# A four-layer conditioned sequence kernel: start of the scans, order of the attention's products, place of the last SiLU

## The chip, the core and the metric

The kernel runs on one core of a Trainium2 chip, in one launch. The metric is the time on the device in microseconds (us), the median of several runs. Engine names are those of the profile: PE multiplies matrices (PEld are its weight loads), DVE, ACT and POOL work on elements, SP issues the DMAs. All data is float32.

## What is computed

Two sequences of 1024 positions with 256 features go through four layers, each with a residual and each shifted and scaled by a condition vector:

```python
x = L0(x, c)     # layer norm, in-projection, conv of 4 taps, SiLU, selective scan, SiLU gate, out-projection
x = L1(x, c)     # two layer norms, two selective scans (one over the reversed sequence), SiLU gates
x = L2(x, e)     # attention with softmaxes over features of q and over positions of k: k^T v first
x = L3(x, e)     # full softmax attention: 16 heads of 16 features over 1024 positions
# a selective scan, for 512 channels x 16 states:
h = h * exp(dt * A) + (dt * u) * B ;  y = sum_n(h * C)
# the end of L2 and L3:
h = layer_norm(y) * (1 + scale) + shift ;  x = x + silu(h) @ W + b
```

## The kernel before

**Order of the work.** The body is written under a manual schedule, which starts at line 1515: each engine runs its instructions in the order in which Python traces them. The constants above it (lines 144 to 203: columns, masks, `negA`, the SiLU of the condition) are placed by the scheduler. Three stages follow each other.

**Prologue.** `layer0(0)` is traced until the first block of dt is saved: layer norm of two tiles of 512 positions (`normed`, with `root` for 1/sqrt by Ln and Exp on ACT, `refine` on DVE, `scaled` on ACT), flips to channels and their eviction with the condition's scale and shift (`channels`), the in-projection and a conv of four taps (three `scalar_tensor_tensor` on DVE for each of four blocks of channels, line 674), SiLU (`smooth`), the projection to dt, B and C (`ssm_inputs`) and softplus. Between the layer norm and the flips stand the condition's matmuls (`cond_first`, `cond_cols`) and their columns (`affine`). ACT needs different tables of functions for SiLU and for Ln and Exp; `preload_act_table_set` (line 203 and line 684) loads one that has both Ln and Exp.

**Scans.** `chain` goes through six scans of 32 pairs of tiles. A tile holds 32 channels x 4 states by 1024 positions. For each: `load_spread` brings dt and dt*u from DRAM (`sp`), `load_bc` B and C (`bc`), ACT makes exp(dt*A) (`decay`, line 931), POOL dt*u*B (`inputs`, line 936), DVE scans (lines 943 and 947) and multiplies with C (line 950) or leaves that to POOL (line 949), and PE sums over states into `ys_t` (`fold`, line 974). Before the first pair, lines 1019 to 1032 load the first tiles in the order spread 0, bc 0, spread 1, bc 1 to 3, and make the first decay and three inputs. The other layers' work is cut into generators that `Behind` runs between the tiles within a budget of matmul columns, ACT and POOL time. `later` and `save` delay a DMA by a number of these slots; in the prologue, `until` issues all that is delayed at its next turn.

**Tail.** `attention` computes L3's softmax attention and runs the last generators behind it. A step handles, for a group of four heads, one tile of 128 keys against 512 queries. It is cut into two parts. In each part PE makes four scores (line 1418): two whose exponentials ACT takes out of PSUM (line 1497) into `hb_t`, and two of a group 12 steps ahead (`LAG`), whose maxima DVE takes (line 1427). Scores go into a pool of seven banks (`sc`); the eighth bank, `av`, collects the products of exponentials with v, 32 rows for each of the four heads. After its scores, each part issues the products of the step before for half of the columns:

```python
for j in range(4):
    at = (j % 2) * 512 + part * 256
    nc.tensor.matmul(
        sums.av[32 * j : 32 * j + 32, ts(part, 256)],
        sts[b]["v"][t // 2][:, t % 2, 4 * g + j, :], es[j // 2][:, at : at + 256],
        start=(t == 0 and part == 0), stop=(t == NT - 1 and part == 1),
    )
```

Then one step of a background generator follows (`behind.slot(1)`), so such work can stand between the halves of a step. When a half of a sequence is done, `last` flips it back, divides by the sums, and `stylize` ends the layer: layer norm, flips, eviction with scale and shift as Identity, SiLU in place over each of two tiles (`channels`, `silu`, which loads the table of Ln and Exp again), the out-projection and the residual (line 791).

The profile gives one line for helpers: L133 is `act_f`, L95 is `mm`, L99 is `flip`, L120 is `save`.

Of the kernel before, what the change touches and what calls it, by code (L numbers as in the profile page):

```python
# [12 lines left out]
AF = mybir.ActivationFunctionType  # L13
# [5 lines left out]
P = 128  # L19
# [35 lines left out]
def kernel(ctx: ExitStack, tc: tile.TileContext, a: dict, out: bass.AP):  # L55
# [146 lines left out]
    act_f(sc, cT, AF.Silu)  # L202
    nc.scalar.preload_act_table_set("natural_log_exp_and_others")

# [48 lines left out]
    def affine(mod, scale_at, shift_at, g, bias, name):  # L253

        s = const.tile([P, 2, B], F32, tag=f"{name}s", name=f"{name}s")
        o = const.tile([P, 2, B], F32, tag=f"{name}o", name=f"{name}o")
        for c in range(2):
            g_c, b_c = col(g, c), col(bias, c)
            at = mod[:, scale_at + c, :]
            act_f(s[:, c, :], at, AF.Identity, bias=g_c, scale=g_c)  # L260
            t = small_t((P, B), "aff")
            act_f(t, mod[:, shift_at + c, :], AF.Identity, bias=b_c)
            for b in range(B):
                act_f(
                    o[:, c, b : b + 1], at[:, b : b + 1], AF.Identity,
                    bias=t[:, b : b + 1], scale=b_c,
                )
        return s, o
# [155 lines left out]

    def scaled(src, r, q):
        o = abuf((P, 4, D))
        for j in range(4 if mode["tail"] else 0):
            nc.vector.tensor_scalar(
                o[:, j, :], src[:, j, :], r[:, j : j + 1], q[:, j : j + 1], ALU.mult, ALU.add
            )  # L430
        for j in range(0 if mode["tail"] else 4):
            act_f(
# [5 lines left out]
    def normed(src, res):  # L438
# [9 lines left out]
        for i, t in enumerate(src):  # L448
            res.append(scaled(t, r[:, ts(i, 4)], q[:, ts(i, 4)]))
            yield  # L450
# [6 lines left out]

    def channels(src, dst, func, scale, bias, halves=(0, 1)):

# [6 lines left out]

        def take(i, c, ps):
            act_f(
                dst[c][:, ts(i, 512)], ps, AF.Identity, bias=bias(c), scale=scale(c)
            )  # L470
# [4 lines left out]
        ))  # L475
        if func is AF.Silu:
            done = slice(512 * halves[0], 512 * halves[-1] + 512)
# [78 lines left out]
    def ssm_inputs(key, u, w_xp, w_dt, dt_b, st):  # L556
# [15 lines left out]
        if key == "00":  # L572
            pss = [bank() for _ in range(2)]
            for k in range(4):
                for ch in range(2):
# [3 lines left out]
                    )  # L579
            take(0, pss[0])  # L580
            nc.vector.tensor_copy(dbl[:, 512:], pss[1][: R + 2 * N, :])
        else:
# [3 lines left out]
        st["bc"] = dbuf((2 * N, T), f"bc_{key}")  # L586
        save(2, st["bc"], dbl[R : R + 2 * N, :])


# [286 lines left out]
    class Scan:  # L876
# [56 lines left out]

        def inputs(self, c, k):
            e = hb()
            nc.gpsimd.tensor_tensor(e, self.sp[c, 1], self.bc[0][k], ALU.mult)  # L936
            return e
# [53 lines left out]
    def chain(scans, rates, early, mid, after):  # L991
# [29 lines left out]
        for w in range(2):  # L1021
            s.load_spread(0, w)
        s.load_bc(0)
        for w in range(2):
# [4 lines left out]
        ahead(0, "decay")  # L1029
        ahead(0, "inputs")  # L1030
        ahead(1, "inputs")
# [62 lines left out]

    def stylize(b, y, aff, w_o, bias, src, dst, halves=(0, 1), to=None):

# [3 lines left out]
        yield from normed(y, yn)  # L1100
        y.clear()
        hT = [abuf() for _ in range(2)]
        yield from channels(
            yn, hT, AF.Silu, lambda c: s[:, c, b : b + 1], lambda c: o[:, c, b : b + 1], halves
        )
# [266 lines left out]
    def last(b, st, src, i):  # L1372
# [22 lines left out]
        ))  # L1395
        yield from stylize(b, y, "aff3", w_o, row("bo3"), src, out[b], (i,))

    def attention(sts, done):
# [50 lines left out]

        def sums(part, n, step, es):  # L1450

            b, g = groups[n]
            ch, t = divmod(step, NT)
            if t == 0 and part == 0:
                sums.av = bank("av")
            for j in range(4):
                at = (j % 2) * 512 + part * 256
                nc.tensor.matmul(  # L1458
                    sums.av[32 * j : 32 * j + 32, ts(part, 256)],
                    sts[b]["v"][t // 2][:, t % 2, 4 * g + j, :], es[j // 2][:, at : at + 256],  # L1460
                    start=(t == 0 and part == 0), stop=(t == NT - 1 and part == 1),
                )
            if t == NT - 1 and part == 1:
                if ch == 0:
# [6 lines left out]
        for at in range(steps + LAG):  # L1471
# [8 lines left out]
            for part in range(2):  # L1480
# [12 lines left out]
                for kind, j, ps in made:  # L1493
                    if kind:
                        top(n1, step1, j, ps)
                    else:
                        act_f(es[j // 2][:, ts(j % 2, 512)], ps, AF.Exp)
                if late is not None:
                    sums(part, *late)
                    if part == 1 and late[0] % 4 == 3 and late[1] % NT == NT - 1:  # L1500
                        done(late[0] // 4, late[1] // NT)
                    if part == 1:
                        late = None
                behind.slot(1)
            if has_e:
                late = (n, step, es)
        for part in range(2):
            sums(part, *late)
        done(B - 1, 1)
# [4 lines left out]
    x3 = [dbuf((T, D), f"x3{b}") for b in range(B)]  # L1514
    ctx.enter_context(tc.manual_schedule())
    sts = [{"v": [], "qk": [], "y": []} for _ in range(B)]
    with ExitStack() as s:
# [4 lines left out]
        psum.append(s.enter_context(tc.tile_pool(name="psS", bufs=1, space=bass.MemoryType.PSUM)))  # L1522
        s00 = Scan("00", negA[0], "D0", False, True)
        s01 = Scan("01", negA[0], "D0", False, True)
        s10 = Scan("10", negA[1], "D1", False, False)
# [194 lines left out]
```

## Time and profile before

| | |
|---|---|
| median of 3 runs | 2122.8 us (2117.06 to 2125.97) |
| profiled execution | 2117.43 us |
| its span, first to last instruction | 2115.4 us |
| busy in the span | PE 1626.8, DVE 1745.5, POOL 1356.9, ACT 1140.4 us |
| granted TensorE clock, mean | 0.833 |
| first scan starts | 69.5 us |
| first and last score | 1479.0 and 2088.6 us |

A row of the profile's timeline is: start in us, duration in us, engine, line, operation, output<-inputs by the program's names, shapes, and how many instructions are merged in it; in brackets how long the engine was idle before it and what ended that. One matmul in float32 stands as two instructions in PE's rows. Ends of PE's rows are modelled, so the distance from the start of one row to the start of the next says more than a row's duration. Parts of the span are named by its time in us.

### The profile page before, as it was taken

The page shows a single profiled execution, that of the slowest core. Times are in us where ns is not written, and L with a number is a line of the kernel's source. Part 1 is how long each engine was busy: PE and PEld are TensorE (multiplying, and loading weights), DVE is VectorE, ACT ScalarE, POOL GpSimd, SP SyncE. Part 2 cuts the span into 40 slices and gives each one's busy share as a digit, 9 for nine tenths or more (in the row PEclk, how much of TensorE's full clock was granted, in tenths as well). Part 3 has the DMA queues.
Part 4 walks back from the last instruction along what each step waited for, and adds up shares of the span by engine and source line. Part 5 has one row for each costly group of instructions (what it writes and reads, how often), then busy time and mean ns, then how long its engine had stood idle before and what let it go on. Part 6 is the DMA issues. An engine that isn't in the chain of part 4 may idle for free.

```text
span 2115.4 us, 22775 instructions
## 1 busy us (share of the span) xinstructions
PE 1626.8 (77%) x8112; PEld 617.7 (29%) x8112; DVE 1745.5 (83%) x1728; ACT 1140.4 (54%) x1583; POOL 1356.9 (64%) x667
## 2 busy tenths in 40 slices
PE   6576867288697547886945658944999899999997
PEld 3132313033141202222312323300545333333333
DVE  4688898898999999998999987998767757777763
ACT  5565666375546345764555453542044555656665
POOL 0789898898999999999998977998101211000000
PEclk9688968599796558988977865965899999999999
DMA  3663458245653555555653344332300111020001
GB/s 111 239 222 114 157 184 292 83 157 185 254 196 141 179 172 187 189 179 188 250 206 110 117 159 144 123 132 73 116 1 1 39 21 18 23 56 1 2 1 38
DMA packets 106870, 267.53 MB, mean 126 GB/s; under 512 B 14618, under 2 KB 39067, under 8 KB 106756
## 3 DMA queue, kind: packets, MB, share of 16 engines
q1 hardware_dynamic: 106756, 266.07, 37.1%
q8 instruction: 64, 1.05, 0.2%
q14 instruction: 50, 0.41, 0.1%
HBM read 195.90 MB, written 67.90 MB: 125 GB/s over the span
## 4 chain that ended last, share of the span: by engine, by line
PE 30%; DVE 10%; POOL 5%; issue 4%; ACT 2%; DMA 0%; DVEq 0%; ACTq 0%; POOLq 0%
PE sc_t L1418 13%; PE av_t L1458 6%; PE sc_t L95 4%; POOL hb_t L936 3%; PE bank_t L95 3%; DVE dA_t L943 2%; DVE mh L1427 2%; PE sc_t L99 2%; DVE dA_t L947 2%; POOL hb_t L949 1%; PE ys_t L974 1%; DVE hb_t L943 1%; ACT act_t L133 1%; POOL act_t L141 1%; DVE hb_t L947 1%
## 5 line engine op out<-in xcount | busy, mean ns | idle before, releaser
L936 POOL TENSOR_TENSOR hb_t<-sp,bc 128x1024 f32<-128x1024 f32 x384 | 908.8, 2399 | 88.5 <-PE ys_t L974 52.0
L133 ACT ACTIVATE dA_t<-sp,negA 128x1024 f32<-128x1024 f32 x384 | 428.5, 1117 | 548.3 <-DVE hb_t L950 432.8
L947 DVE TENSOR_TENSOR_SCAN dA_t<-dA_t,hb_t 128x1024 f32<-128x1024 f32 x195 | 445.9, 2287 | 62.3 <-ACT dA_t L133 35.1
L1427 DVE TENSOR_REDUCE mh<-sc_t 128x1 f32<-128x512 f32 x512 | 327.5, 686 | 110.2 <-PE sc_t L1418 109.8
L974 PE MATMUL ys_t<-hb_t,fold 128*32 128x512 f32 x1536 | 294.2, 781 | 153.5 <-POOL hb_t L949 101.1
L133 ACT ACTIVATE hb_t<-sc_t 128x512 f32<-128x512 f32 x512 | 276.9, 595 | 188.7 <-PE sc_t L1418 188.5
L950 DVE TENSOR_TENSOR hb_t<-dA_t,bc 128x1024 f32<-128x1024 f32 x285 | 349.1, 1225 | 21.4 <-DVE dA_t L947 0.5
L1418 PE MATMUL sc_t<-act_t 32*128 32x512 f32 x2048 | 336.6, 650 | 11.0 <-DVE mh L1427 7.3
L949 POOL TENSOR_TENSOR hb_t<-hb_t,bc 128x1024 f32<-128x1024 f32 x99 | 235.7, 2381 | 19.6 <-DVE hb_t L947 17.8
L784 POOL TENSOR_TENSOR act_t<-act_t,row 128x1024 f32<-128x1024 f32 x8 | 18.7, 2347 | 339.9 <-PE sc_t L99 193.3
L943 DVE TENSOR_TENSOR_SCAN dA_t<-dA_t,hb_t 128x1024 f32<-128x1024 f32 x90 | 205.7, 2285 | 9.2 <-POOL hb_t L936 6.0
L1458 PE MATMUL av_t<-hb_t,act_t 128*32 128x256 f32 x2048 | 164.3, 393 | 1.1 <-DVE act_t L1466 1.1
L95 PE MATMUL bank_t<-act_t,w_c_w 128*128 128x512 f32 x256 | 129.6, 657 | 41.2 <-ACT act_t L133 41.2
L133 ACT ACTIVATE act_t<-bank_t,cols 128x512 f32<-128x512 f32 (+1 forms) x206 | 129.9, 677 | 44.5 <-PE bank_t L95 38.7
L1418 PEld LDWEIGHTS sc_t<-act_t 32*128 32x128 f32 x2048 | 111.1, 185 | 120.9 <-issue 79.9
L974 PEld LDWEIGHTS ys_t<-hb_t,fold 128*32 128x32 f32 x1536 | 40.5, 123 | 358.9 <-POOL hb_t L949 139.5
L947 DVE TENSOR_TENSOR_SCAN hb_t<-dA_t,hb_t 128x1024 f32<-128x1024 f32 x61 | 139.0, 2279 | 3.9 <-ACT dA_t L133 3.6
L141 POOL TENSOR_TENSOR act_t<-act_t 128x1024 f32<-128x1024 f32 x50 | 118.4, 2367 | 0.2
L99 PE MATMUL bank_t<-ident,act_t 128*128 128x128 f32 x128 | 34.6, 426 | 92.5 <-ACT act_t L133 92.3
L95 PE MATMUL bank_t<-act_t,w_dt_w 64*128 64x512 f32 x96 | 74.6, 912 | 40.4 <-ACT act_t L133 34.4
L1458 PEld LDWEIGHTS av_t<-hb_t,act_t 128*32 128x32 f32 x2048 | 42.1, 108 | 190.5 <-issue 177.8
L1363 POOL MEMSET act_t<- 128x1024 f32 x8 | 7.6, 952 | 128.0 <-PE sc_t L1418 128.0
(176 smaller groups left out, 1833.9 us busy)
## 6 DMA issues: line engine op xcount, KB each, us to landing
sp<-dt SPq DMA_DIRECT2D x192, 512.0 KB, 5.3
dt<-act_t SPq DMA_DIRECT2D x48, 512.0 KB, 5.2
bc<-bc SPq DMA_DIRECT2D x48, 512.0 KB, 7.7
u<-act_t SPq DMA_DIRECT2D x24, 512.0 KB, 5.0
fu<-u SPq DMA_DIRECT2D x24, 512.0 KB, 4.5
y<-y SPq DMA_DIRECT2D x96, 128.0 KB, 5.8
g<-act_t SPq DMA_DIRECT2D x16, 512.0 KB, 5.3
fg<-g SPq DMA_DIRECT2D x64, 128.0 KB, 4.7
```

What stands on the lines that cost most here:

```text
L95: nc.tensor.matmul(o, w, x, **kw)
L133: nc.scalar.activation(o, x, func, **kw)
L141: nc.gpsimd.tensor_tensor(o, x, y, op)
L936: nc.gpsimd.tensor_tensor(e, self.sp[c, 1], self.bc[0][k], ALU.mult)
L943: nc.vector.tensor_tensor_scan(h[:, ::-1], dA[:, ::-1], e[:, ::-1], 0.0, ALU.mult, ALU.add)
L947: nc.vector.tensor_tensor_scan(h, dA, e, 0.0, ALU.mult, ALU.add)
L949: return lambda: nc.gpsimd.tensor_tensor(e, h, self.bc[1][k], ALU.mult)
L950: nc.vector.tensor_tensor(e, h, self.bc[1][k], ALU.mult)
L974: nc.tensor.matmul(self.ys[d, cp][at : at + DS, :], fold, e[:, ts(ch, 512)], start=False, stop=(k == NK - 1),)
L1418: nc.tensor.matmul(ps, w[r, ts(at, P)], x[r, ts(wide_at, 512)], start=True, stop=True)
L1427: nc.vector.tensor_reduce(mh[n][:, t, ch, j : j + 1], ps, AX.X, ALU.max)
L1458: nc.tensor.matmul(sums.av[32 * j : 32 * j + 32, ts(part, 256)], sts[b]["v"][t // 2][:, t % 2, 4 * g + j, :], es[j // 2][:, at : at + 256] ...
```

## The change

It has three parts. In the prologue, the preload of the table moves from behind the condition's SiLU to the first place under the manual schedule; while no scans run yet, the columns of `affine`, the scaling of the second tile, the eviction of the second block of channels and both copies of the projection are done by DVE instead of ACT; the load of the first B and C is issued behind their save, before dt is saved; the first product dt*u*B is made by DVE. In the attention, the products of the step before are issued once a step, behind the second part's scores, over 512 columns. In the very last `stylize`, a SiLU of one column is issued after the layer norm, the eviction applies SiLU itself, and the separate SiLUs and the reload of the table are left out.

```diff
--- before.py
+++ after.py
@@ -200,7 +200,6 @@
 
     sc = const.tile([P, 4, B], F32, tag="sc", name="sc")
     act_f(sc, cT, AF.Silu)
-    nc.scalar.preload_act_table_set("natural_log_exp_and_others")
 
     def small_t(shape, tag, bufs=2):
         return small.tile(list(shape), F32, tag=tag, name=tag, bufs=bufs)
@@ -257,6 +256,14 @@
         for c in range(2):
             g_c, b_c = col(g, c), col(bias, c)
             at = mod[:, scale_at + c, :]
+            if not mode["scans"]:
+                t = small_t((P, B), "aff")
+                nc.vector.tensor_scalar(t, at, 1.0, None, ALU.add)
+                nc.vector.tensor_scalar(s[:, c, :], t, g_c, None, ALU.mult)
+                nc.vector.scalar_tensor_tensor(
+                    o[:, c, :], t, b_c, mod[:, shift_at + c, :], ALU.mult, ALU.add
+                )
+                continue
             act_f(s[:, c, :], at, AF.Identity, bias=g_c, scale=g_c)
             t = small_t((P, B), "aff")
             act_f(t, mod[:, shift_at + c, :], AF.Identity, bias=b_c)
@@ -422,13 +429,14 @@
         e.scalar_tensor_tensor(q, mv[:, :, 0], -1.0, r, ALU.mult, ALU.mult)
         return q
 
-    def scaled(src, r, q):
+    def scaled(src, r, q, i):
         o = abuf((P, 4, D))
-        for j in range(4 if mode["tail"] else 0):
+        far = mode["tail"] or i and not mode["scans"]
+        for j in range(4 if far else 0):
             nc.vector.tensor_scalar(
                 o[:, j, :], src[:, j, :], r[:, j : j + 1], q[:, j : j + 1], ALU.mult, ALU.add
             )
-        for j in range(0 if mode["tail"] else 4):
+        for j in range(0 if far else 4):
             act_f(
                 o[:, j, :], src[:, j, :], AF.Identity,
                 bias=q[:, j : j + 1], scale=r[:, j : j + 1],
@@ -446,7 +454,7 @@
         q = refine(mv, r)
         yield
         for i, t in enumerate(src):
-            res.append(scaled(t, r[:, ts(i, 4)], q[:, ts(i, 4)]))
+            res.append(scaled(t, r[:, ts(i, 4)], q[:, ts(i, 4)], i))
             yield
 
     def silu(t):
@@ -455,7 +463,7 @@
         nc.scalar.preload_act_table_set("natural_log_exp_and_others")
         spent["ACT"] += 2400
 
-    def channels(src, dst, func, scale, bias, halves=(0, 1)):
+    def channels(src, dst, func, scale, bias, halves=(0, 1), ready=False):
 
 
         def turn(i, c):
@@ -465,15 +473,21 @@
             return ps
 
         def take(i, c, ps):
+            if c and not (mode["scans"] or mode["tail"]):
+                nc.vector.tensor_scalar(
+                    dst[c][:, ts(i, 512)], ps, scale(c), bias(c), ALU.mult, ALU.add
+                )
+                return
             act_f(
-                dst[c][:, ts(i, 512)], ps, AF.Identity, bias=bias(c), scale=scale(c)
+                dst[c][:, ts(i, 512)], ps, func if ready else AF.Identity,
+                bias=bias(c), scale=scale(c),
             )
 
         yield from pipe(*(
             (lambda i=i, c=c: turn(i, c), lambda ps, i=i, c=c: take(i, c, ps))
             for i in halves for c in range(2)
         ))
-        if func is AF.Silu:
+        if func is AF.Silu and not ready:
             done = slice(512 * halves[0], 512 * halves[-1] + 512)
             act_f(dst[0][:, done], dst[0][:, done], func)
             silu(dst[1][:, done])
@@ -577,14 +591,16 @@
                         pss[ch][: R + 2 * N, :], w_xp[:, k, :], u[k][:, ts(ch, 512)],
                         start=(k == 0), stop=(k == 3),
                     )
-            take(0, pss[0])
-            nc.vector.tensor_copy(dbl[:, 512:], pss[1][: R + 2 * N, :])
+            for ch in range(2):
+                nc.vector.tensor_copy(dbl[:, ts(ch, 512)], pss[ch][: R + 2 * N, :])
         else:
             yield from pipe(*(
                 (lambda ch=ch: low(ch), lambda ps, ch=ch: take(ch, ps)) for ch in range(2)
             ))
         st["bc"] = dbuf((2 * N, T), f"bc_{key}")
         save(2, st["bc"], dbl[R : R + 2 * N, :])
+        if "first" in st:
+            later(2, st["first"])
 
 
         st["dt"] = dbuf((2, DI, T), f"dt_{key}")
@@ -931,9 +947,9 @@
             act_f(dA, self.sp[c, 0], AF.Exp, scale=self.nA[:, at : at + 1])
             return dA
 
-        def inputs(self, c, k):
+        def inputs(self, c, k, engine=nc.gpsimd):
             e = hb()
-            nc.gpsimd.tensor_tensor(e, self.sp[c, 1], self.bc[0][k], ALU.mult)
+            engine.tensor_tensor(e, self.sp[c, 1], self.bc[0][k], ALU.mult)
             return e
 
         def tile(self, c, k, dA, e, far=False):
@@ -1020,14 +1036,13 @@
         behind.until(lambda: s.st["have"])
         for w in range(2):
             s.load_spread(0, w)
-        s.load_bc(0)
         for w in range(2):
             s.load_spread(1, w)
         for k in range(1, NK):
             s.load_bc(k)
         s.load_rest(0)
         ahead(0, "decay")
-        ahead(0, "inputs")
+        made["inputs"][0] = s.inputs(0, 0, nc.vector)
         ahead(1, "inputs")
         ahead(2, "inputs")
         mode["scans"] = True
@@ -1092,16 +1107,20 @@
         scans[-1].finish(3, 1)
         flush()
 
-    def stylize(b, y, aff, w_o, bias, src, dst, halves=(0, 1), to=None):
+    def stylize(b, y, aff, w_o, bias, src, dst, halves=(0, 1), to=None, at_end=False):
 
         s, o = cond[aff]
         xt, bias = load_src(src, bias, halves)
         yn = []
         yield from normed(y, yn)
         y.clear()
+        if at_end:
+
+            act_f(small_t((P, 1), "kmx"), one, AF.Silu)
         hT = [abuf() for _ in range(2)]
         yield from channels(
-            yn, hT, AF.Silu, lambda c: s[:, c, b : b + 1], lambda c: o[:, c, b : b + 1], halves
+            yn, hT, AF.Silu, lambda c: s[:, c, b : b + 1], lambda c: o[:, c, b : b + 1], halves,
+            at_end,
         )
         yield from residual(
             hT, w_o, xt, bias, dst, range(2 * halves[0], 2 * halves[-1] + 2)
@@ -1393,7 +1412,9 @@
             (lambda t=t: turn(t), lambda ps, t=t: divide(t, ps))
             for t in range(4 * i, 4 * i + 4)
         ))
-        yield from stylize(b, y, "aff3", w_o, row("bo3"), src, out[b], (i,))
+        yield from stylize(
+            b, y, "aff3", w_o, row("bo3"), src, out[b], (i,), at_end=(b, i) == (B - 1, 1)
+        )
 
     def attention(sts, done):
 
@@ -1447,20 +1468,19 @@
         tops = abuf((P, 4, P), pool=act)
         nc.gpsimd.memset(tops, 0.0)
 
-        def sums(part, n, step, es):
+        def sums(n, step, es):
 
             b, g = groups[n]
             ch, t = divmod(step, NT)
-            if t == 0 and part == 0:
+            if t == 0:
                 sums.av = bank("av")
             for j in range(4):
-                at = (j % 2) * 512 + part * 256
                 nc.tensor.matmul(
-                    sums.av[32 * j : 32 * j + 32, ts(part, 256)],
-                    sts[b]["v"][t // 2][:, t % 2, 4 * g + j, :], es[j // 2][:, at : at + 256],
-                    start=(t == 0 and part == 0), stop=(t == NT - 1 and part == 1),
+                    sums.av[32 * j : 32 * j + 32, :],
+                    sts[b]["v"][t // 2][:, t % 2, 4 * g + j, :], es[j // 2][:, ts(j % 2, 512)],
+                    start=(t == 0), stop=(t == NT - 1),
                 )
-            if t == NT - 1 and part == 1:
+            if t == NT - 1:
                 if ch == 0:
                     sts[b]["y"].append(abuf())
                 nc.vector.tensor_copy(sts[b]["y"][-1][:, ts(ch, 512)], sums.av)
@@ -1495,17 +1515,15 @@
                         top(n1, step1, j, ps)
                     else:
                         act_f(es[j // 2][:, ts(j % 2, 512)], ps, AF.Exp)
-                if late is not None:
-                    sums(part, *late)
-                    if part == 1 and late[0] % 4 == 3 and late[1] % NT == NT - 1:
+                if part == 1 and late is not None:
+                    sums(*late)
+                    if late[0] % 4 == 3 and late[1] % NT == NT - 1:
                         done(late[0] // 4, late[1] // NT)
-                    if part == 1:
-                        late = None
+                    late = None
                 behind.slot(1)
             if has_e:
                 late = (n, step, es)
-        for part in range(2):
-            sums(part, *late)
+        sums(*late)
         done(B - 1, 1)
         while behind.queue or behind.soon:
             behind.slot(1)
@@ -1513,6 +1531,7 @@
     x2 = [dbuf((T, D), f"x2{b}") for b in range(B)]
     x3 = [dbuf((T, D), f"x3{b}") for b in range(B)]
     ctx.enter_context(tc.manual_schedule())
+    nc.scalar.preload_act_table_set("natural_log_exp_and_others")
     sts = [{"v": [], "qk": [], "y": []} for _ in range(B)]
     with ExitStack() as s:
         bcp, spread, fin, yp = [
@@ -1521,6 +1540,7 @@
         ]
         psum.append(s.enter_context(tc.tile_pool(name="psS", bufs=1, space=bass.MemoryType.PSUM)))
         s00 = Scan("00", negA[0], "D0", False, True)
+        s00.st["first"] = lambda: s00.load_bc(0)
         s01 = Scan("01", negA[0], "D0", False, True)
         s10 = Scan("10", negA[1], "D1", False, False)
         s20 = Scan("20", negA[2], "D2", True, True, s10)
```

## The prediction, before the change was run

> **What bounds the kernel now.** I read the busy time by stage first, then the timeline of one attention step, then the prologue and the end. The columns of the stage view are stretch, length, busy us of PE, PEld, DVE, ACT, POOL, granted clock, DMA share and GB/s.
>
> ```profile
> 69.50:1479.00 1409.50, 979.67 (x3300) 349.01 (x3300) 1283.99 (x882) 770.03 (x927) 1295.86 (x618) 0.77 0.50 170
> ...
> 1755.00:2052.00 297.00, 293.34 (x2597) 103.13 (x2596) 227.64 (x391) 179.88 (x326) 14.59 (x7) 1.00 0.07 16
> ```
>
> The scans (69.5 to 1479) are held by DVE and POOL at 91% each. The diff leaves their loop alone, so they only move with their start. In the attention tail PE is busy for 293 of 297 us at a clock of 1.00, DVE for 77%, ACT for 61%: there a change of PE's order shows at once. One step of it, on all engines:
>
> ```profile
> 1987.24 1.14 PE L1418 MATMUL sc_t<-act_t 32*128 32x512 f32 x8
> 1988.31 0.64 PE L1458 MATMUL av_t<-hb_t,act_t 128*32 128x256 f32 x8
> 1988.44 1.29 DVE L1427 TENSOR_REDUCE mh<-sc_t 128x1 f32<-128x512 f32 x2 [0.63 <-PE sc_t L1418]
> 1988.46 1.09 ACT L133 ACTIVATE hb_t<-sc_t 128x512 f32<-128x512 f32 x2 [0.84 <-PE sc_t L1418]
> 1988.88 0.52 PEld L1418 LDWEIGHTS sc_t<-act_t 32*128 32x128 f32 x8 [0.41 <-issue]
> 1988.88 1.35 PE L1418 MATMUL sc_t<-act_t 32*128 32x512 f32 x8
> 1990.16 0.64 PE L1458 MATMUL av_t<-hb_t,act_t 128*32 128x256 f32 x8
> ```
>
> Four scores run side by side (eight rows, two passes each). By starts: 1.07 us of scores, 0.57 of products with v, 1.28, 0.57: 3.49 a step. The two groups of scores have the same work, yet one takes 0.21 more. The loads of its weights spread over 0.52 instead of 0.31 us: its fourth score starts late. The pool has seven score banks and a step makes eight scores, so the fourth of a group takes the bank of the first of the group before. That one is free when its exponential ends: scores end at 1988.31, ACT starts 0.15 later and takes 0.60, and PE follows some 0.05 after. This is a distance of 0.80 from the end of one group to the start of the next group's fourth. The products cover 0.57 of it, and the 0.21 is the rest. The 256-column products between the halves are thus also the cover of a wait.
>
> **The tail's change.** It takes away two groups of products of 256 columns and puts one of 512 behind both halves. How much PE needs for it is shown where both halves run on end already:
>
> ```profile
> 2054.58 1.07 PE L1458 MATMUL av_t<-hb_t,act_t 128*32 128x256 f32 x16
> 2055.58 1.14 PE L1418 MATMUL sc_t<-act_t 32*128 32x512 f32 x8
> ```
>
> The next row starts 1.00 later, against 2 x 0.57 = 1.14. Two 512-column passes would be 2 x 0.48 (0.24 for 256 columns) + 0.09 = 1.05; I take 1.02 and keep 1.00 and 1.05. Without a wait a step would be 1.07 + 1.07 + 1.02 = 3.16, so -0.33. But now the second half follows the first directly. Its fourth score starts 0.80 after the first half's end and takes 1.07 itself, and the products, which need the whole array, wait behind it. The step becomes 1.07 + 0.80 + 1.07 + 1.02 = 3.96, +0.47. DVE (4 x 0.65) and ACT (4 x 0.55) fit in that; no later bank is late, since 1.02 of products stand before the next step's first half.
>
> The Trainium skill speaks on both sides here (TensorEngine Tiling (Array Packing)). Its section Key Properties says that a change of tiling mode drains the engine, and the change halves these; the rows give 0.12 a step for it. Its section PSUM Bottleneck says that tiling speeds the matmuls and not the emptying of PSUM. By the first alone the step would be 3.16, by the second 3.96; the late fourth score in the row decides for the second.
>
> How many steps: in PE's timeline from 1547 to 2054 I count 114. In 82 nothing else of PE lies between the halves: +0.47 each. In 14 four flips of 0.59 lie there, leaving 0.21 of wait: +0.21 - 0.12 = +0.09. In 18 background matmuls of 1.1 to 2.0 us hide it all: -0.12. Sum 38.5 + 1.3 - 2.2 = +37.6. About 5 come off: some old groups took 1.36 to 1.96 because DVE was late, and a longer step gives DVE its time (the 78 steps from 1755 on take 299.4 now and 327.5 at the new prices). **Tail: +32.5.** Bounds: with a distance of 0.70 (the four scores' releases a little earlier) 8 less; with 1.05 for the products and nothing absorbed, 9 more.
>
> **The prologue.**
>
> ```profile
> 8.55 7.61 PE L95 MATMUL bank_t<-sc,act_t 128*128 128x2 f32 x32 [8.55 <-DMA act_t<-in_ada_w]
> 16.02 1.95 PE L99 MATMUL bank_t<-ident,act_t 128*128 128x128 f32 x8
> 21.32 1.97 PE L99 MATMUL bank_t<-ident,act_t 128*128 128x128 f32 x8 [3.35 <-ACT act_t L133]
> 23.08 5.51 PE L95 MATMUL dA_t<-act_t,w_in_w 128*128 128x512 f32 x11
> ```
>
> Between Ln (11.57) and Exp of rstd ACT has two loads of tables of 1.28 us. One table instead would take 2.6 off ACT. But PE is busy with the condition's matmuls until 16.02 and the flips stand behind them, so this saves at most 0.3; if that cover were gone, 2.6. The preload has no operands, and the old one (L203) ran at 0.78, ahead of the SiLU written above it. Should the new one do the same, the two loads stay, and it costs those 0.3. The same cover hides the second tile's scaling on DVE (4 x 0.41 beside ACT's 4 x 0.5). Behind 16.02 it counts: eight ACT rows for the affine columns, 18.18 to 20.51, become six on DVE, starting at 16.36 at 0.20 each (the L419 to L422 rows): 17.6. Evictions are then ACT at 17.1 (0.76) and DVE at 18.0 (0.75, as L602 from PSUM); the second flips end at 19.65, where they ended at 23.08. **-3.4.** Both copies of the projection on DVE (0.69 against ACT's 0.58 plus the wait for its table) leave PE's next matmul where it is: 0.
>
> Then the first products. SP's issues, and POOL's rows:
>
> ```profile
> 57.98 2.19 SPq L899 DMA_DIRECT2D sp<-dt  x2
> 60.25 1.20 SPq L889 DMA_DIRECT2D bc<-bc  x2
> 61.51 1.75 SPq L899 DMA_DIRECT2D sp<-dt  x2
> ```
>
> ```profile
> 67.14 2.34 POOL L936 TENSOR_TENSOR hb_t<-sp,bc 128x1024 f32<-128x1024 f32 x1 [10.15 <-DMA bc<-bc]
> 70.87 4.70 POOL L936 TENSOR_TENSOR hb_t<-sp,bc 128x1024 f32<-128x1024 f32 x2 [1.39 <-DMA sp<-dt]
> ```
>
> The first sp lands at 61.8 (ACT's decay starts), the fourth at 70.87: five landings in 9.1 us, 1.8 each. The two bc transfers go ahead of them, behind the save of bc (issued 49.28, landed 2.7 later). SP waits there with nothing behind it before the save of dt at 55.34; on the DMA engines that save can queue behind them by up to 0.9, for which I charge 0.3. With both out of the way the fourth sp lands 3.6 earlier. The first product moves to DVE (1.23, as L950) in the gap before its first scan, and POOL starts its chain with the second product 3.3 earlier: **-3.3** (2 to 3.8), on top of the -3.4. POOL is at 95% from 69.5 to 100, so the scans follow it. Prologue: **-6.7**, kept through the scans, which have only relative waits.
>
> **The end.**
>
> ```profile
> 2102.15 1.58 ACT L133 ACTIVATE act_t<-sc_t,aff3o,aff3s 128x512 f32<-128x512 f32 x2 [2.82 <-PE sc_t L99]
> 2103.75 1.28 ACT L133 ACT_TABLE_LOAD   x1
> 2105.04 1.15 ACT L133 ACTIVATE act_t<-act_t 128x512 f32<-128x512 f32 x2
> ```
>
> The table moves into ACT's idle 2.82; SiLU in the eviction ends at 2103.73, and PE starts 0.04 later instead of at 2105.73: **-2.0**. The Trainium skill (ScalarE: Activation LUTs, section What ACT_TABLE_LOAD costs) puts a switch at 1.28 plus a drain of 1.38; here the next activation starts 1.29 after the load, so there is no drain to win, and -3.3 by the page becomes -2.0 by the row.
>
> **The rivals.** (1) No bank wait: the fourth score finds its bank free, or other work covers the wait in most steps. For it: the weight loads of a group can run early, and PE's row shows no idle time. Against: the 0.21 is in every undisturbed step. It would give 82 x -0.33 - 32 x 0.12 = -31 for the tail, and -40 in all: 2083. The point from which the sign turns is a wait of about 0.5 us a step. (2) A wait near that point, the prologue and end making up for the rest: 2112 to 2133. (3) The mechanism and more: PE's holes lower its clock. The stretch with holes before 1755 has 0.94; 6% on 3.16 us of 82 steps is +15: 2162. (4) The prologue's edits don't take effect (the preload floats ahead, the dt save is held by the loads): half of the -6.7 is lost, 2150.
>
> **The numbers.** The profiled execution took 2117.43 (span 2115.4). -6.7 + 32.5 - 2.0 = +23.8 makes 2141.2; the median of the runs is 5.4 above the profiled one, so 2146. Chances: mechanism as summed, with (3) and (4), 0.75, its own range 2130 to 2162; (2) 0.13; (1) 0.12. The range reaches down to 2114 for most of (2). A measurement here tells about 0.5% (10.6 us) from no change. Faster 0.12, within 0.20 (case (2) and the low end of the first), slower 0.68.
>
> **What would show it.** In the tail the rows of PE should read sixteen L1418, then eight L1458 of 512 columns, with a step of about 3.95 us, the last two score passes late and alone; DVE and ACT busy shares fall. PE starts the first conv matmuls near 19.7, POOL its first product near 64, and one table load stands in ACT's gap at the end. I am wrong if the sixteen scores of a step take about 2.1 us, or if the first scan does not come 6 to 8 us earlier.

## The result, and the profile after

The changed kernel took 2148.61 us (median of 4 runs, 2147.95 to 2150.51) beside 2119.93 for the kernel before (4 runs): a ratio of 1.0116, interval 1.0083 to 1.0150. A second measurement, of ten runs, gave 2138.69 beside 2122.68, a ratio of 1.0078 (1.0050 to 1.0107). Both say slower: the ratios make it 17 to 25 us, the medians 16 to 29. The first profiled execution took 2150.51 with a span of 2148.5.

By stage, between the same events of both profiles (the second scan's start, the last scan's start, the copy of the last products with v, the end), the span of the kernel before is 73.3 + 1399.3 + 620.3 + 22.5, and that of the changed one 67.9 + 1411.1 + 650.2 + 19.2. The prologue gave 5.4, the end 3.3, the tail took 29.9. The 11.8 by which the scans differ lie within their scatter from execution to execution, which the table behind the experiments shows.

The stage view of the changed kernel (stretch, length, busy us of PE, PEld, DVE, ACT, POOL, clock, DMA share, GB/s), for the scans and for the undisturbed part of the tail:

```profile
67.94:1484.60 1416.66, 986.09 (x3301) 349.66 (x3299) 1280.90 (x880) 764.73 (x922) 1304.40 (x617) 0.77 0.49 169
1770.00:2090.00 320.00, 318.29 (x1969) 105.67 (x1968) 220.49 (x387) 171.06 (x323) 14.58 (x7) 1.00 0.05 15
```

PE counts as busy for 318 of 320 us at a clock of 1.00, as before, although it now waits in every undisturbed step: a group of four scores of which three are done and one waits is one busy row. DVE's share fell from 77% to 69%, ACT's from 61% to 53%. The busy share of the bound engine doesn't show the loss; the shares of the two engines that it feeds do. One step on all engines shows where it is:

```profile
2020.14 2.99 PE L1439 MATMUL sc_t<-act_t 32*128 32x512 f32 x16
2020.67 0.20 PEld L1439 LDWEIGHTS sc_t<-act_t 32*128 32x128 f32 x3 [0.22 <-issue]
2021.10 0.20 PEld L1439 LDWEIGHTS sc_t<-act_t 32*128 32x128 f32 x3 [0.23 <-issue]
...
2021.36 2.06 ACT L133 ACTIVATE hb_t<-sc_t 128x512 f32<-128x512 f32 x4 [1.85 <-PE sc_t L1439]
2022.00 0.29 PEld L1439 LDWEIGHTS sc_t<-act_t 32*128 32x128 f32 x2 [0.70 <-ACT hb_t L133]
...
2023.06 1.07 PE L1478 MATMUL av_t<-hb_t,act_t 128*32 128x512 f32 x8
2024.05 0.71 PE L1439 MATMUL sc_t<-act_t 32*128 32x512 f32 x4
```

The first half's scores end at about 2021.21 (2020.14 and the 1.07 that a half took before; the row of all sixteen does not show it). Three scores of the second half load their weights in threes, from 2020.67 on. The fourth pair of loads stands at 2022.00, released by ACT's exponential: 0.80 after the first half's end. The products begin at 2023.06, one full score pass later, and the next step at 2024.05. So 2.92 + 1.00 = 3.92 a step, where the prediction had 3.96. In the view of waits (us in total, times, longest), the scores' weight loads waited for an exponential in the tail of the kernel before, of the changed one, and of `seven_merged`, a kernel of the experiments below:

```profile
PEld sc_t L1418 <- ACT hb_t L133: 4.8, 15, 0.7
PEld sc_t L1439 <- ACT hb_t L133: 65.7, 96, 1.0
PEld sc_t L1439 <- ACT hb_t L133: 57.7, 76, 0.8
```

The count alone proves no wait of PE: the undisturbed steps of `seven_merged` have none, and most of its 76 are idle time of the weight loads while PE is in the products. It is the late pair of loads inside the scores (2022.00), together with the step's length, that shows the wait.

In the prologue PE, SP, POOL and DVE now read:

```profile
16.28 4.11 PE L99 MATMUL bank_t<-ident,act_t 128*128 128x128 f32 x16
20.18 8.30 PE L95 MATMUL dA_t<-act_t,w_in_w 128*128 128x512 f32 x16
...
53.07 2.00 SPq L120 DMA_DIRECT2D dt<-act_t  x2
55.72 3.48 SPq L915 DMA_DIRECT2D sp<-dt  x4
...
65.48 4.75 POOL L952 TENSOR_TENSOR hb_t<-sp,bc 128x1024 f32<-128x1024 f32 x2 [10.76 <-DMA sp<-dt]
67.94 2.30 DVE L963 TENSOR_TENSOR_SCAN dA_t<-dA_t,hb_t 128x1024 f32<-128x1024 f32 x1 [1.00 <-POOL hb_t L952]
```

Two rows of the kernel before, for the same in-projection and the same second scan:

```profile
23.08 7.65 PE L95 MATMUL dA_t<-act_t,w_in_w 128*128 128x512 f32 x16
...
73.30 2.30 DVE L947 TENSOR_TENSOR_SCAN dA_t<-dA_t,hb_t 128x1024 f32<-128x1024 f32 x1 [0.23 <-POOL hb_t L936]
```

All sixteen flips are one group, and the in-projection starts at 20.18 instead of 23.08. Its sixteen rows take 8.30 instead of 7.65, so part of the gain is lost again. The second product dt*u*B, POOL's first now, starts at 65.48, against 70.87. The first scan comes at 63.38 instead of 69.51, 6.1 earlier, and the second 5.4 earlier. And ACT's loads of tables, in the first 14 us:

```profile
0.78 1.28 ACT L1534 ACT_TABLE_LOAD   x1 [0.78 <-PEq L1729]
...
3.56 1.28 ACT L133 ACT_TABLE_LOAD   x1
...
10.96 1.28 ACT L133 ACT_TABLE_LOAD   x1 [5.89 <-DVE mv L402]
...
12.57 1.28 ACT L133 ACT_TABLE_LOAD   x1
```

There is no "one table": the SiLU's load at 3.56 is followed by both loads, for Ln and for Exp. The preload itself (L1534, written behind the SiLU) stands at 0.78, ahead of everything. At the end, first PE before, then ACT and PE now:

```profile
2100.62 2.30 PE L99 MATMUL sc_t<-ident,act_t 128*128 128x128 f32 x8 [5.31 <-DVE act_t L428]
2105.73 5.75 PE L95 MATMUL sc_t<-w_vo_w,act_t 128*128 128x256 f32 x16 [2.81 <-ACT act_t L133]
```

```profile
2135.68 1.28 ACT L133 ACT_TABLE_LOAD   x1
...
2136.95 2.30 PE L99 MATMUL sc_t<-ident,act_t 128*128 128x128 f32 x8 [5.29 <-DVE act_t L436]
...
2138.48 1.58 ACT L133 ACTIVATE act_t<-sc_t,aff3o,aff3s 128x512 f32<-128x512 f32 x2 [1.30 <-issue]
...
2139.31 5.23 PE L95 MATMUL sc_t<-w_vo_w,act_t 128*128 128x256 f32 x16
```

The load lies in ACT's gap, and PE starts 0.05 after the first of the two evictions (2138.48 + 0.78), not after the second.

### The profile page after: what moved, and what is told of

The parts are those of the page before. It is cut to its first block, busy times and chain, and to the rows that moved or that the text cites. A ratio compares the mean times of both kernels' runs of the same rounds, so it can differ in the third digit from the quotient of the medians.

```text
span 2148.5 us, 20714 instructions
## 1 busy us (share of the span) xinstructions
PE 1667.6 (78%) x7088; PEld 620.8 (29%) x7088; DVE 1747.6 (81%) x1742; ACT 1123.4 (52%) x1566; POOL 1365.6 (64%) x666
## 5 line engine op out<-in xcount | busy, mean ns | idle before, releaser
L133 ACT ACTIVATE hb_t<-sc_t 128x512 f32<-128x512 f32 x512 | 269.9, 600 | 225.4 <-PE sc_t L1439 225.2
L1439 PE MATMUL sc_t<-act_t 32*128 32x512 f32 x2048 | 380.9, 647 | 8.7 <-DVE mh L1448 4.9
L1439 PEld LDWEIGHTS sc_t<-act_t 32*128 32x128 f32 x2048 | 134.1, 188 | 205.8 <-ACT hb_t L133 65.7
L963 DVE TENSOR_TENSOR_SCAN hb_t<-dA_t,hb_t 128x1024 f32<-128x1024 f32 x61 | 139.0, 2278 | 4.8 <-ACT dA_t L133 4.0
L1478 PE MATMUL av_t<-hb_t,act_t 128*32 128x512 f32 x1024 | 140.5, 615 | 0.0
L959 DVE TENSOR_TENSOR_SCAN hb_t<-dA_t,hb_t 128x1024 f32<-128x1024 f32 x38 | 86.6, 2280 | 2.5 <-ACT dA_t L133 2.5
```

What stands on the lines that cost most here:

```text
L133: nc.scalar.activation(o, x, func, **kw)
L959: nc.vector.tensor_tensor_scan(h[:, ::-1], dA[:, ::-1], e[:, ::-1], 0.0, ALU.mult, ALU.add)
L963: nc.vector.tensor_tensor_scan(h, dA, e, 0.0, ALU.mult, ALU.add)
L1439: nc.tensor.matmul(ps, w[r, ts(at, P)], x[r, ts(wide_at, 512)], start=True, stop=True)
L1478: nc.tensor.matmul(sums.av[32 * j : 32 * j + 32, :], sts[b]["v"][t // 2][:, t % 2, 4 * g + j, :], es[j // 2][:, ts(j % 2, 512)], start=(t ...
```

## The experiments

**Which part carries the change.** Theory: the products' place costs about 31, prologue and end give 7 and 3 back. Rival: the early scores or the prologue's moved work cost it. Three kernels took one part of the diff each onto the kernel before, and a fourth took prologue and end together. `products` is the hunks of `sums` and its call:

```diff
-                    sums.av[32 * j : 32 * j + 32, ts(part, 256)], ..., es[j // 2][:, at : at + 256],
+                    sums.av[32 * j : 32 * j + 32, :], ..., es[j // 2][:, ts(j % 2, 512)],
-                if late is not None:
-                    sums(part, *late)
+                if part == 1 and late is not None:
+                    sums(*late)
```

> The kernel before with the tail's part alone: products of 512 columns once a step, behind both halves' scores. Theory of the bank wait (the eighth score of a step waits for the bank of the first): an undisturbed step of attention 3.92 us instead of 3.49, +29 to +32 us in all, 2149 to 2152. Rival, that the loss of the changed kernel lies elsewhere (in the scans, which took 11.8 us more in its profile): +18 to +20 us or less.

Measured: 2148.14, ratio 1.0130 (1.0086 to 1.0173). The tail is 642.7 long (620.3 before), and its undisturbed steps repeat at 3.92. Over an undisturbed half of a group, eight steps from one copy of `av` to the next, it takes 31.9 us, the changed kernel 32.0, the kernel before 28.6. That the whole tail is 7.5 shorter than the changed kernel's comes from its first groups and its last half, and was not followed up. `prologue` is the diff without these hunks and without the last SiLU:

> The kernel before with the prologue's part alone. Theory (the start moves forward by 5.4 us at the second scan, and waits in the scans are relative): -5 us, 2115. Rival (the 11.8 us that the scans took more in the changed kernel's profile come with the shifted start): +2 to +7 us, and the first score as late as in the changed kernel.

Measured: 2114.63 over 22 runs, ratio 0.9973 (0.9955 to 0.9992). `end` is only the SiLU in the eviction and the one-column SiLU ahead of it (`at_end` and `ready`):

> The kernel before with the end's part alone: the last SiLU in the eviction, its table loaded ahead. Both theories: -3.3 us (from the last copy of av to the last instruction 19.2 us instead of 22.5), near what a comparison can tell.

Measured: 2118.31, ratio 0.9990 (0.9970 to 1.0010); the part behind the last products is 18.8 instead of 22.5. These runs can't tell 3 us from nothing, the profile can. `prologue_end` is the changed kernel with the products back in two halves:

```diff
-                if part == 1 and late is not None:
-                    sums(*late)
+                if late is not None:
+                    sums(part, *late)
```

> The changed kernel with its products put back in two halves of 256 columns, one behind each half's scores; prologue and end as changed. Theory of the bank wait: 2119.9 - 5.4 - 3.3 = 2111, faster than both kernels. Rival (the scans lose by the shifted start): 2118 to 2123.

Measured: 2107.76 over 22 runs, ratio 0.9943 (0.9922 to 0.9964). This version is faster than both kernels. So the loss is the products', and the other two parts are no loss. The changed kernel ran again beside the next kernels:

> The changed kernel once more, in the same rounds as the runs beside it: 2147 to 2150. Theory: its steps of attention take 3.92 us (2.92 for sixteen scores, 1.00 for the products) and its scans between 1398 and 1411 us, as in all kernels.

Measured: 2138.69, ratio 1.0078 (1.0050 to 1.0107), ten runs from 2124.71 to 2147.02, so below the expected 2147 to 2150; steps of 3.92 and a tail of 650.4, the same as the first time to 0.2.

**Width or place.** Does the 512-column form cost it, or that the products stand behind both halves? `place` keeps the 256 columns of before and only moves both groups behind the second half:

```diff
-                if late is not None:
-                    sums(part, *late)
+                if part == 1 and late is not None:
+                    for half in range(2):
+                        sums(half, *late)
```

> The kernel before with its products still of 256 columns, but both halves of them behind the second half's scores. Theory of the bank wait (the place counts, not the width): step 3.92 us, +28 us, 2147 to 2150. Rival (wide products themselves are slow, or long groups of them hold PE): step near 3.5 us, 2120.

Measured: 2148.19, ratio 1.0120 (1.0084 to 1.0156). PE's timeline:

```profile
2046.55 2.99 PE L1418 MATMUL sc_t<-act_t 32*128 32x512 f32 x16
2049.47 1.07 PE L1458 MATMUL av_t<-hb_t,act_t 128*32 128x256 f32 x16
2050.47 2.99 PE L1418 MATMUL sc_t<-act_t 32*128 32x512 f32 x16
```

By starts 2.92 and 1.00, as with 512 columns. So the width of the products doesn't matter here; their place does.

**Banks, or late exponentials.** If seven banks for eight scores are the cause, a step of seven scores must not wait, and merging must then gain. Head 3's maxima are taken from head 2's scores here, so one score and its two passes are left out; everything else stays, the eviction too. `seven_merged` does this to the changed kernel, `seven_halves` to the kernel before:

```diff
+                            if kind and js[i] == 3:
+                                made.append((kind, 3, made[-2][2]))
+                                continue
```

> The changed kernel with seven scores a step instead of eight: head 3's maximum is taken a second time from another head's scores, so its own score for the maxima is left out; DVE and ACT do as much as before. Theory of the bank wait: with seven scores and seven banks no score waits for one of the same step, a step is 1.07 + 1.07 + 1.00 = 3.14 us, -64 us against the changed kernel, 2085. Rival (PE's own work in this order is slow): at most an eighth of the scores' time, which costs PE nothing where four run side by side, 2140 to 2149.

> The kernel before with the same score left out. Theory of the bank wait: only the 0.21 us goes, a step is 1.07 + 0.57 + 1.07 + 0.57 = 3.28 us, -17 us, 2103: so without the wait the order turns, and the products of 512 columns are the faster by some 18 us. Rival: as far below the kernel before as the other is below the changed one, so that the halves stay ahead by 28 us.

Measured: merged 2073.17, ratio 0.9776 (0.9741 to 0.9810); halves 2103.21, ratio 0.9908 (0.9880 to 0.9935). Merged first, then halves:

```profile
1989.62 1.99 PE L1439 MATMUL sc_t<-act_t 32*128 32x512 f32 x14
1991.54 1.06 PE L1478 MATMUL av_t<-hb_t,act_t 128*32 128x512 f32 x8
1992.54 0.66 PE L99 MATMUL sc_t<-ident,act_t 128*128 128x128 f32 x4
1993.12 2.99 PE L1439 MATMUL sc_t<-act_t 32*128 32x512 f32 x14
1996.04 1.07 PE L1478 MATMUL av_t<-hb_t,act_t 128*32 128x512 f32 x8
```

```profile
2005.99 1.14 PE L1418 MATMUL sc_t<-act_t 32*128 32x512 f32 x8
2007.06 0.64 PE L1458 MATMUL av_t<-hb_t,act_t 128*32 128x256 f32 x8
2007.63 1.13 PE L1418 MATMUL sc_t<-act_t 32*128 32x512 f32 x6
2008.69 0.64 PE L1458 MATMUL av_t<-hb_t,act_t 128*32 128x256 f32 x8
2009.26 1.14 PE L1418 MATMUL sc_t<-act_t 32*128 32x512 f32 x8
```

With seven scores a step is 1.92 + 1.00 = 2.92 merged, and 1.07 + 0.57 + 1.06 + 0.57 = 3.27 in halves. The order of the two forms turns: merging now gains 0.35. Both kernels leave out the same work of PE, so less work alone doesn't turn it. The flips in the merged kernel are a second test, which no expectation names: where four of them take an eighth bank (1992.54), the same fourteen rows take 2.92 again, and the last pair of weight loads is late again (at 1994.99, behind an exponential). So seven banks keep eight scores from the gain of merging.

The merged time is 12 below what I wrote, and one reason is the scores: I had put them at 1.07 + 1.07 = 2.14, and on end, with nothing between the halves, seven of them take 1.92. By the profiles, the merged kernel's tail is 584.7 against 650.2 and its scans happened to be 11.1 shorter than in the changed kernel's first profile.

**What the prologue's parts give.** Two kernels take the 5.4 apart. `one_table` is prologue_end with the preload held where it is written:

```diff
-    nc.scalar.preload_act_table_set("natural_log_exp_and_others")
+    tc.keep_in_program_order(
+        nc.scalar.preload_act_table_set("natural_log_exp_and_others")
+    )
```

> prologue_end with its table load held in its place behind the condition's SiLU, so that the prologue really has one table for Ln and Exp. In the profile of after the load had floated to 0.78 us and two loads, at 10.96 and 12.57, stayed. My theory: the rows' statistics are ready about 1.3 to 2.6 us earlier, but TensorE is in the condition's products until about 16.0, so the first flips still start at 16.0 to 16.3 and nothing later moves by more than 0.3 us: a ratio to before within 0.003 of prologue_end's 0.9943. Rival: ScalarE's loads held the statistics and so the flips; then the flips and the evictions start 1 to 2.6 us earlier, and the second scan starts at 64 to 65.5 instead of 66.7.

Measured: 2110.96, ratio 0.9945 (0.9921 to 0.9969): the ratio of prologue_end. Ln and Exp of rstd follow each other now, at 10.26 and 10.59, without a load; in ACT's view of prologue_end they stood at 11.80 and 13.42. On PE:

```profile
11.64 5.71 PE L95 MATMUL bank_t<-sc,act_t 128*128 128x2 f32 x26 [0.26 <-DMA act_t<-in_ada_w]
17.21 3.97 PE L99 MATMUL bank_t<-ident,act_t 128*128 128x128 f32 x16
```

The rows are scaled by 13.7, and the flips start when the condition's products end: at 17.21, because the products' weights came later in this execution (PE starts at 9.58, in prologue_end at 8.30). For this reason and another one (the loads of dt and u follow the save of dt by 3.77, in prologue_end by 2.83) the second scan came at 69.5, so the expected 0.3 could only be tested by the ratio. The two loads of tables, however real on ACT, cost no time that the ratio shows as long as PE is in those products. `bc_ahead` is the kernel before with the early load of B and C and the first product on DVE:

```diff
+        if "first" in st:
+            later(2, st["first"])
...
-        s.load_bc(0)
...
-        ahead(0, "inputs")
+        made["inputs"][0] = s.inputs(0, 0, nc.vector)
```

> The kernel before with two edits of the prologue alone: the first load of B and C ahead of the stores of dt, and the first scan's product with B on VectorE. The flips and evictions are as before. My theory: the prediction gave these edits 3.3 of the prologue's 6.7, so the second scan starts 2.5 to 3.5 us ahead of the 73.3 to 74.7 that the kernels without the prologue's part show: at 70.0 to 71.5. Rival: the evictions carry it all, and the second scan stays at 73 to 74.5.

Measured, in one execution: 2118.23; the second scan starts at 71.37, POOL's first product of its own at 68.92. That is 1.9 ahead of the 73.30 and 70.87 of the kernel before, whose first matmul behind the evictions starts at the same time (23.08, here 23.09), and 2.6 to 3.3 ahead of the other kernels with the old prologue (73.9 to 74.7).

**A version that lets the scores run by sevens.** If the banks decide, the whole computation should gain from it too when no group needs an eighth bank. `sevens` queues the scores and issues them seven at a time, each run followed by the products that are due (the flips of the maxima and the background steps move along with it):

```diff
+        def seven():
+            now = [pend.pop(0) for _ in range(min(7, len(pend)))]
...
+            made = [(v, score(v[2], v[3], v[1], v[0])) for v in now]
+            while ready and ready[0][0] < count[0]:
...
+                sums(at_n, at_step, es)
```

> The changed kernel with its whole computation, but its scores issued in runs of seven, as many as there are banks, instead of eight a step; behind each run's scores come the four products of 512 columns of the step whose last exponential the run before held. So nothing between two runs of scores has to wait for a bank as long as seven scores and four products last longer than an eviction. My theory: a step costs eight sevenths of the 1.92 that fourteen rows took with seven scores, and 1.00 for the products, 3.19 in place of 3.49 with the products in two halves; over 114 steps up to 34 below prologue_end, less where VectorE is late or a run has no products: 2074 to 2096, a ratio to before of 0.978 to 0.989. Rival: the price of merging is not the banks but the late exponentials; then a step stays near 3.9 and the time above 2140.

Measured: 2117.63 over 20 runs, ratio 0.9977 (0.9955 to 0.9999). It does away with the change's loss (tail 616.4 from first score to last copy, the changed kernel 644.7), but it is no better than prologue_end (613.6), and the expected 2074 to 2096 was a miss. PE's timeline shows where it loses:

```profile
2016.76 1.99 PE L1439 MATMUL sc_t<-act_t 32*128 32x512 f32 x14
2018.68 1.06 PE L1477 MATMUL av_t<-hb_t,act_t 128*32 128x512 f32 x8
2019.68 4.40 PE L1439 MATMUL sc_t<-act_t 32*128 32x512 f32 x28
2024.01 1.06 PE L1477 MATMUL av_t<-hb_t,act_t 128*32 128x512 f32 x8
```

A run of seven costs 1.92 where products stand on both sides. But eight steps need a little over nine runs and have eight groups of products, so two runs meet: 4.33 for 28 rows, 0.49 more than twice 1.92. The run that starts at 2009.65 takes 3.13. It is the first after the last products of a half of a group, and DVE copies those out at 2009.79 for 0.69 before the maxima, for which PE's weight loads wait at 2011.13 and 2011.72. From copy to copy of `av`, the eight steps of this half took 27.6 us here and 28.6 in prologue_end. In the last group, which has exponentials and no maxima, sevens takes 25.0 for the first half against 21.4. Gains of up to 1.0 in the calm halves and such losses cancel.

**What an execution adds by itself.** The scans' loop is the same in all these kernels. From the second to the last scan the profiles show, in us:

| kernel | second scan at | scans | last scan to last copy | end |
|---|---|---|---|---|
| before | 73.3 | 1399.3 | 620.3 | 22.5 |
| changed | 67.9 | 1411.1 | 650.2 | 19.2 |
| changed, again | 67.1 | 1408.0 | 650.4 | 19.2 |
| products | 74.5 | 1400.2 | 642.7 | 22.3 |
| prologue | 68.8 | 1408.1 | 620.6 | 23.4 |
| end | 74.3 | 1404.1 | 620.6 | 18.8 |
| prologue_end | 66.7 | 1397.7 | 619.7 | 18.8 |
| place | 73.9 | 1405.7 | 646.5 | 22.4 |
| seven_merged | 68.2 | 1400.0 | 584.7 | 19.2 |
| seven_halves | 74.7 | 1412.0 | 601.5 | 22.8 |
| one_table | 69.5 | 1412.3 | 620.9 | 18.6 |
| bc_ahead | 71.4 | 1401.4 | 620.1 | 23.3 |
| sevens | 67.8 | 1399.8 | 622.7 | 18.9 |

The second scan starts at 73.3 to 74.7 in the five kernels with the old prologue (mean 74.1) and at 66.7 to 69.5 in the seven with the new one (mean 68.0). The scans scatter from 1397.7 to 1412.3. Among the longest is one with the old prologue (seven_halves, 1412.0), and the shortest has the new one (prologue_end). The means are 1403.8 for the six kernels with the old prologue or the early B and C alone, and 1405.3 for the seven with the new one. So no lengthening by the prologue's edits is seen, and the 11.8 of the first comparison lie within the scatter. What makes an execution take the longer course was not found.

## Why the prediction was right, step by step

- **The mechanism of the tail was right, and so was its size.** Prediction: +32.5 from a distance of 0.80, a step of 3.96. Measured: distance 0.80, step 3.92 (the scores 2.92 where the sum has 2.94, the products 1.00 where it has 1.02), tail +29.9 from the last scan and +30.8 from the first score (613.9 to 644.7). Over the 82 undisturbed steps 0.04 is 3.3, and the tail was 2.6 too high. `place` shows that the place does it, the two `seven` kernels that it is the banks.
- **"Without a wait a step would be 1.07 + 1.07 + 1.02 = 3.16, so -0.33"** was wrong, though the seven kernels differ by 0.35. The -0.33 was the old wait of 0.21 and 0.12 on the products. In the seven kernels the halves have no such wait: the 0.35 is 0.14 on the products (2 x 0.57 - 1.00) and 0.21 on the scores, which take 1.92 on end and not 2.13. That the two numbers agree is luck. By the same rows, eight scores with a free bank would make a step of about 2.92, which is an estimate from seven. The forecast didn't suffer: with the wait, the fourth score's pass stands alone, and the sum for that case holds.
- **"Two 512-column passes would be 1.05; I take 1.02"** was a little too much: 512 columns and twice 256 take the same 1.00 when nothing stands between (changed, and place). What is saved on the products is the passage between the two kinds of tile, not the width.
- **The prologue, -6.7: measured -5.4, by the means of the table -6.1.** The flips and evictions were put at -3.4. They gave 2.9, with PE's first condition product 0.22 later in this execution (8.77 against 8.55). Then the in-projection's rows took 0.65 longer (8.30 against 7.65; in prologue_end 7.66, and why they differ was not found), so that the save of dt and the first loads of dt and u came only 2.26 earlier. The load of B and C and the first product were put at -3.3. They gave the rest, 5.4 - 2.26 = 3.1, and by bc_ahead alone 1.9 to 3.3. My 0.3 for a delay of the save of dt was not spent here: the loads follow the save by 2.65, before by 2.64. In prologue_end it is 2.83, in bc_ahead 3.06, in one_table 3.77.
- **The preload: "should the new one do the same, the two loads stay".** It did, and they did. That this costs nothing that can be seen was right too, since one_table removes them and gains nothing. One reading was off: of the two loads before, one stands ahead of Ln (10.28) and one between Ln and Exp (11.89), not both between. Likewise POOL's share in the scans was 92%, not 91%.
- **The end, -2.0: measured -3.3.** The step that failed is "SiLU in the eviction ends at 2103.73 and PE starts 0.04 later". PE's first products need only the first of the two tiles, so they start after one eviction. From the start of the last flips PE's wait fell from 5.11 (2100.62 to 2105.73) to 2.36 (2136.95 to 2139.31), which is 2.0 and one eviction of 0.78. The last products took 5.23 instead of 5.75 as well; in end and prologue_end they took 4.8, and the cause stays open. The drain of 1.38, which the Trainium skill (ScalarE: Activation LUTs, section What ACT_TABLE_LOAD costs) adds to a switch, is not what makes up the -3.3: the one-column SiLU runs at 2136.97, 1.29 after the load's start.
- **The sum.** -5.4 + 29.9 - 3.3 = +21.2, against +23.8 predicted. The prologue missed by +1.3 and the end by -1.3, so they cancel, which is luck; what is left is the tail's 2.6. The two ratios, 17 to 25, hold both. The first median (2148.61) came nearer to 2146 than the second (2138.69). The one execution of the first four that has a profile had long scans; whether the other three had is not shown.
- **The rivals.** (1), no bank wait, fell by the late pair of loads and by the two seven kernels. (2), a wait near 0.5, fell: the wait was 0.80, and a step cost 0.43 net. (3), a lower clock from PE's holes, was not seen in the undisturbed part, at 1.00 before and after. Over the whole tail the clock was 0.97 before and 0.96 after. (4) came true in one half (the preload floats ahead) and without its price; the other half, the save of dt held by the loads, did not happen in this execution.

## What to carry to other kernels

Count the results that are under way on PE between two groups of other work, and the banks they go to: if there is one more result than banks, whatever stands between the halves covers a release (here 0.80 us: 0.15 to start, 0.60 to empty, 0.05 back), and moving it away uncovers all of it. Look for the late one in the timeline of the weight loads, since the matmul row of the group counts as busy; a sum of the loads' waits also counts idle time under other work of PE. Merge passes of another tile mode only where the number under way fits in the banks, and test that by leaving one result out: if both versions lose the same work and their order turns, it was the banks.

## What was not expected of the hardware

- Eight products of 512 columns and sixteen of 256, on end, take the same 1.00 us; two passages between the tile modes fewer in a step save 0.14 (1.14 - 1.00). The Trainium skill (TensorEngine Tiling (Array Packing), section Key Properties) says that a change of mode drains the engine; worked out from these rows, an estimate, that is about 0.07 us a change.
- The same loop of scans took 1397.7 to 1412.3 us in thirteen profiled executions, and the kernel before ran from 2111 to 2137 us over 113 runs. The end's 3.3 us show in its profile, and not in the comparison of 22 runs with 59 (0.9970 to 1.0010).
- A load of a table without operands stood at 0.78 us, ahead of an activation that is written ahead of it, and two more loads followed behind that activation; held in its place, it stood at 5.28 and both later loads were gone.
